# Gating and adding the last expert results: VectorE alone, or VectorE and ScalarE

## The chip, the cores and the metric

The kernel runs on one core of a Trainium2 chip. The metric is the device time of one execution in microseconds (us). Six runs of the kernel before gave a median of 709.76 us (706.66 to 710.63).

A core has five engines with instruction queues of their own: TensorE (PE in the profile, its weight loads PEld), VectorE (DVE), ScalarE (ACT), GpSimd (POOL) and SyncE (SP, which here only issues transfers). They wait for each other and for DMA transfers by semaphores.

## What is computed

A "macaron" block over x, 8 sequences of 512 tokens of width 128, in float32: half a mixture of experts, attention, and half a mixture of experts again. The last line below is the one that the change belongs to.

```
def ffn(x):                                   # 8 experts, each token goes to 2
    logits = einsum('bsd,de->bse', x, router_w) + router_b
    topk_scores, topk_idx = top_k(logits, 2)
    topk_gates = softmax(topk_scores, axis=-1)
    combine = einsum('bsk,bske->bse', topk_gates, one_hot(topk_idx, 8))
    ...                                       # over the experts:
        h = relu(einsum('bsd,df->bsf', x, w1) + b1)        # 128 -> 512
        y = einsum('bsf,fd->bsd', h, w2) + b2              # 512 -> 128
        acc = acc + y * combine_e[..., None]

x = x + 0.5 * ffn(layernorm(x))
x = x + attention(layernorm(x))               # 16 heads of 8, causal
x = x + 0.5 * ffn(layernorm(x))
```

Every token thus receives two results of the second mixture of experts, one from each of its two experts. Each is multiplied by the token's gate for that expert, and both are added to x. The gates already hold the factor 0.5.

## The kernel before

All of x stays on the chip: `x[b]` is a tile of 128 partitions x 4 x 128 for sequence b. Token t*128 + p of the sequence is in partition p, at index t. "A tile of tokens" below is one such t: 128 tokens, one in each partition, 128 values each.

**The groups.** The tokens go through the mixtures of experts in groups. The first mixture has the groups f0, f1 and f2, the second g0, g1 and g2. A group's tokens are routed, normalised and scattered to a buffer in HBM by expert; the experts then fetch their rows, and the results go back to HBM. For g1 and g2 they go there by the token's own place (`send`, L981, by indirect transfers of GpSimd): the buffer `ys` holds for every token two neighbouring rows, the results r = 0 and r = 1.

**The shares of g2.** g2 is the last group. Its tokens lie in four shares: tile 3 of sequence 4, and all four tiles of the sequences 5, 6 and 7. That makes 13 tiles of tokens.

**The order.** The kernel is written as generators, which a plan calls in turn. Attention of all 8 sequences, the experts of the groups and the routing are woven together. The order of the instructions on TensorE, ScalarE, VectorE and SyncE is the order in which they are called. When the last experts of g2 are through, only `collect` is left to do, for the four shares of g2:

```
last = [m.collect(g2, i, out, parts=min(2, g2.shares[i][2] - g2.shares[i][1])) for i in range(4)]
step(*last)
run(*last)
```

`step` takes each of the four generators up to its first `yield`: SyncE issues all loads. `run` then runs the generators one after the other to their end: the arithmetic, and the stores.

**`collect`.** It reads the two rows of every token of a share from `ys` to a tile `yr` (128 partitions x tiles x 2 x 128), in `parts` pieces. For the one-tile share parts is 1, and there is one load; for the others parts is 2, so n is 2, and there are two loads of two tiles of tokens each. All in all seven loads (L1140). Then, for each tile of tokens and for r = 0 and r = 1, VectorE does one fused operation (L1144, `scalar_tensor_tensor`): yr times the gate, a column of one value for each partition, plus x, into x. After the last tile of a part, SyncE stores that part of x to the output (L1150): seven stores. Two shares each use one buffer, `pair`, which stands under the tag "ee" in a pool of two.

The groups before g2 use `collect` as well (g1, with parts = 1), or `combine` (L1098), and have the rest of the kernel to run beside.

After the last store each engine reads a flag, `bad` (L1577), and jumps over a general path (L1581), which runs only for inputs that the fast path can't hold.

Of the kernel before, what the change touches and what calls it, by code (L numbers as in the profile page):

```python
# [14 lines left out]
AF = mybir.ActivationFunctionType  # L15
ALU = mybir.AluOpType
# [471 lines left out]
class Main:  # L488
# [638 lines left out]
    def collect(self, g, i, dst, parts=1):  # L1127

        nc = self.nc
        b, first, end = g.shares[i]  # L1130
        x = self.x[b]
        gates = self.ways[g.key[0], b][2]
        if i % 2 == 0:
            self.pair = self.p2.tile([P, 2, T, 2, D], FP, tag="ee", name=f"yr_{b}")
        yr = self.pair[:, i % 2]
        src = g.ys[: 2 * P * g.tiles, :].rearrange("(t p r) d -> p t r d", p=P, r=2)
        n = -(-(end - first) // parts)
        for t in range(first, end, n):
            rows = slice(t - first + g.base[i], t - first + g.base[i] + n)
            nc.sync.dma_start(yr[:, t : t + n], src[:, rows])  # L1140
        yield
        for t in range(first, end):
            for r in range(2):
                nc.vector.scalar_tensor_tensor(  # L1144
                    x[:, t, :], yr[:, t, r], gates[:, t, r : r + 1], x[:, t, :],
                    ALU.mult, ALU.add,
                )
            if (t - first) % n == n - 1:
                part = slice(t + 1 - n, t + 1)
                nc.sync.dma_start(  # L1150
                    dst[b].rearrange("(t p) d -> p t d", p=P)[:, part], x[:, part]
                )
            if parts == 1:
                yield
# [474 lines left out]
```

## Time and profile before

| | us |
|---|---|
| median of six runs | 709.76 |
| lowest and highest run | 706.66, 710.63 |
| the profiled execution, its whole time | 708.01 |
| its span, from the first instruction to the last | 706.3 |
| TensorE busy | 623.1 (88% of the span) |
| VectorE busy | 406.2 (58%) |
| ScalarE busy | 341.7 (48%) |
| GpSimd busy | 295.0 (42%) |

The granted clock of TensorE was 0.975 of its full speed on average.

How such a profile is read: the profile page has the busy share of each engine in 40 equal slices of the span, one digit for each slice, in tenths. The groups put together the instructions of one line, engine and shape: output, inputs and sizes, how often they ran, then busy time and the mean ns of one, and how long the engine was idle just before them and for whom. The timeline lists instructions in the order of time: start, duration, engine, line, operation. Equal ones in a row are merged, with their number at the end. The chain that ended last goes back from the last instruction of the span to what released it, and so on; its pieces are shown with start and duration. "issue" in it is time in which the engine waited for nothing that the profile shows. The table by windows has for each stretch the busy time and number of instructions of the engines PE, PEld, DVE, ACT and POOL, then the clock of TensorE, the mean share of time in which the core's 16 DMA engines were busy, and the GB/s that they moved.

### The profile page before, as it was taken

What the parts mean: (1) busy time and instruction counts of PE and PEld (TensorE: products, weight loads), DVE (VectorE), ACT (ScalarE), POOL (GpSimd) and SP (SyncE); (2) the same over time, 40 slices, a digit from 0 to 9 for tenths busy, and PEclk for the clock granted to TensorE, in tenths of its full rate; (3) what the DMA queues carried; (4) which work ended last, traced back from release to release, by engine and by line L of the source; (5) the groups of instructions that cost most, each with busy time, mean ns of one, the idle gap of its engine ahead of it and who ended that gap; (6) DMA issues with size and microseconds to landing.
All of it is one profiled execution on the core that took longest, in us unless ns stands there. A gap on an engine that the chain in (4) does not pass through costs nothing.

```text
span 706.3 us, 12906 instructions
## 1 busy us (share of the span) xinstructions
PE 623.1 (88%) x4797; PEld 403.2 (57%) x4797; DVE 406.2 (58%) x1432; ACT 341.7 (48%) x552; POOL 295.0 (42%) x318
## 2 busy tenths in 40 slices
PE   3269979989999999999999999989999988779970
PEld 2148856755656656555656556455465556647760
DVE  6636437644466575675676677767665644233424
ACT  4024443355565656466566565666646532234420
POOL 3744627643132214315054324332244455645550
PEclk9999999999999999999999999999999998979995
DMA  8746843221518961011211101012112121244224
GB/s 263 190 134 200 214 109 93 67 62 53 121 27 128 179 218 37 23 26 46 65 32 50 46 25 38 27 35 80 46 32 62 31 58 38 71 118 131 78 67 150
DMA packets 80229, 61.32 MB, mean 87 GB/s; under 512 B 7400, under 2 KB 73888, under 8 KB 80160
## 3 DMA queue, kind: packets, MB, share of 16 engines
q1 hardware_dynamic: 71296, 42.79, 24.2%
q0 software_dynamic: 8576, 17.63, 8.4%
q8 instruction: 40, 0.66, 0.4%
q14 instruction: 29, 0.24, 0.1%
q10 hardware_dynamic: 288, 0.01, 0.0%
HBM read 26.21 MB, written 34.19 MB: 86 GB/s over the span
## 4 chain that ended last, share of the span: by engine, by line
PE 81%; DVE 5%; ACT 3%; DMA 2%; another core or an unknown queue 2%; issue 2%; POOL 0%; POOLq 0%; SPq 0%; ACTq 0%
PE st L1231 13%; PE y_f L1037 11%; PE o L1257 11%; PE z_f L1013 11%; PE z_g L1013 10%; PE y_g L1037 9%; PE qkv_ps_a L1169 3%; PE qT_ps L1208 2%; PE otok_ps L1275 2%; PE kT_ps L1208 2%; PE xbT_ps_g L1000 2%; PE xbT_ps_f L1000 1%; ACT ee L1238 1%; DVE x L1144 1%
## 5 line engine op out<-in xcount | busy, mean ns | idle before, releaser
L1238 ACT ACTIVATE ee<-st 128x768 f32<-128x768 f32 (+1 forms) x192 | 159.0, 881 | 97.1 <-PE st L1231 84.3
L479 POOL DMA_INDIRECT yt_f<-ys,back_f x64 | 65.1, 1017 | 132.2 <-DVE ee L1245 56.7
L1245 DVE TENSOR_TENSOR ee<-ee,keep 128x256 f32<-128x256 f32 (+1 forms) x192 | 93.4, 507 | 22.7 <-ACT ee L1238 21.6
L1037 PEld LDWEIGHTS y_f<-w_sb,h_f 128*120 128x120 f32 (+1 forms) x704 | 86.0, 182 | 30.0 <-issue 17.1
L1231 PE MATMUL st<-qT,kT 32*128 32x512 f32 (+3 forms) x1024 | 96.1, 467 | 6.7 <-ACT kT L1214 4.3
L895 POOL DMA_INDIRECT xs<-xn_g,to_g x64 | 63.7, 995 | 87.5 <-DVE ee L1245 33.6
L1037 PEld LDWEIGHTS y_g<-w_sb,h_g 128*128 128x128 f32 x640 | 81.6, 193 | 32.5 <-issue 25.9
L1037 PE MATMUL y_f<-w_sb,h_f 128*120 128x128 f32 (+1 forms) x704 | 94.4, 277 | 1.4 <-ACT h_f L1020 1.1
L1013 PE MATMUL z_g<-xT_g,w_sb 128*128 128x512 f32 (+1 forms) x192 | 89.5, 552 | 6.4 <-ACT xT_g L1004 6.4
L1013 PE MATMUL z_f<-xT_f,w_sb 128*128 128x480 f32 (+1 forms) x192 | 89.3, 553 | 1.0 <-ACT xT_f L1004 1.0
L1257 PE MATMUL o<-ee,vpad 128*32 128x512 f32 (+3 forms) x1024 | 89.4, 442 | 0.8 <-DVE ee L1245 0.8
L1020 ACT ACTIVATE h_f<-z_f,b1T 128x480 f32<-128x480 f32 (+1 forms) x86 | 53.5, 625 | 71.6 <-PE z_f L1013 52.4
L1037 PE MATMUL y_g<-w_sb,h_g 128*128 128x128 f32 x640 | 86.1, 280 | 0.6 <-DVE o_tok L1280 0.3
L981 POOL DMA_INDIRECT ys<-ysb_g,home_g x64 | 62.7, 980 | 55.2 <-ACT h_g L1020 16.8
L1020 ACT ACTIVATE h_g<-z_g,b1T 128x512 f32<-128x512 f32 (+1 forms) x77 | 49.3, 642 | 53.4 <-PE z_g L1013 45.6
L1041 DVE TENSOR_TENSOR ysb_g<-y_g,b_sb 128x128 f32<-128x128 f32 x80 | 23.0, 290 | 85.3 <-PE y_g L1037 62.2
L1041 DVE TENSOR_TENSOR ysb_f<-y_f,b_sb 120x128 f32<-120x128 f32 (+1 forms) x88 | 25.0, 288 | 75.5 <-PE y_f L1037 62.5
L1231 PEld LDWEIGHTS st<-qT,kT 32*128 32x128 f32 x1024 | 43.1, 183 | 40.2 <-ACT kT L1214 12.8
L895 POOL DMA_INDIRECT xs<-xn_n,to_f x40 | 38.8, 971 | 36.8 <-issue 9.9
L1257 PEld LDWEIGHTS o<-ee,vpad 128*32 128x32 f32 x1024 | 23.5, 108 | 52.4 <-issue 6.6
L1013 PEld LDWEIGHTS z_g<-xT_g,w_sb 128*128 128x128 f32 x192 | 29.9, 194 | 26.2 <-issue 13.1
L1013 PEld LDWEIGHTS z_f<-xT_f,w_sb 128*128 128x128 f32 x192 | 30.5, 195 | 14.0 <-issue 8.5
(185 smaller groups left out, 770.7 us busy)
## 6 DMA issues: line engine op xcount, KB each, us to landing
xs<-zeros SPq DMA_DIRECT2D x8, 520.0 KB
xb_g<-xs SPq DMA_DIRECT2D x16, 260.0 KB
w_sb<-in_L_ffn_W_dram SPq DMA_DIRECT2D x16, 256.0 KB
xb_f<-xs SPq DMA_DIRECT2D x16, 240.0 KB
ys<-ysb_f SPq DMA_DIRECT2D x16, 240.0 KB
ys<-zeros SPq DMA_DIRECT2D x2, 1664.0 KB
x<-in_L_attn_x_dram SPq DMA_DIRECT2D x8, 256.0 KB
xs<-zeros SPq DMA_DIRECT2D x1, 1920.0 KB
```

The source lines that it names most:

```text
L479: ins = op(*args, **kw)
L895: ins = nc.gpsimd.indirect_dma_start(out=g.xs[:, :], out_offset=bass.IndirectOffsetOnAxis(ap=to[:, t, r : r + 1], axis=0), in_=xn[:, t, : ...
L981: ins = nc.gpsimd.indirect_dma_start(out=g.ys[:, :], out_offset=bass.IndirectOffsetOnAxis(ap=home[e][:rows, t : t + 1], axis=0), in_=ys[:r ...
L1013: nc.tensor.matmul(z[:, :n], self.w1_sb[:, e, ts(c, P)], xT[:, n0 : n0 + n], start=True, stop=True,)
L1020: ins = nc.scalar.activation(dst, z[:, :n], AF.Relu, bias=bias)
L1037: nc.tensor.matmul(y[:rows], h[:, c, ts(t, rows)], self.w2_sb[:, e, c, :], start=(c == 0), stop=(c == C - 1),)
L1041: ins = nc.vector.tensor_tensor(ys[:rows, t, :], y[:rows], self.b2_sb[:rows, e], ALU.add)
L1208: self.nc.tensor.transpose(tp[:, ts(t, P)], pad[:, t, 4 * g : 4 * g + 4, :].rearrange("p h s -> p (h s)"), self.ident,)
L1231: nc.tensor.matmul(st[:, h, c0 : c0 + N - kt * P], kT[r0 : r0 + SLOT, ts(kt, P)], qT[r0 : r0 + SLOT, kt * P :], start=True, stop=True,)
L1238: nc.scalar.activation(ee[:, two, :width], st[:, two, :width], AF.Exp)
L1245: ins = self.nc.vector.tensor_tensor(d, d, self.keep.unsqueeze(1).unsqueeze(1).to_broadcast([P, 2, len(parts), P]), ALU.min,)
L1257: self.nc.tensor.matmul(self.o[h * SLOT : (h + 1) * SLOT, kt * P :], self.vpads[b % 2][:, kt, 4 * g + h, :], ee[:, h, c0 : c0 + n], start= ...
```

## The change

For shares that come in two parts (three of g2's four, 12 of its 13 tiles), the result r = 0 is no longer gated and added by VectorE. ScalarE multiplies it by its gate, in place in `yr`. VectorE still gates and adds the result r = 1 of every tile with its fused operation. After the last tile of a part, one addition of VectorE brings both tiles' gated r = 0 results into x at once, and then the part is stored as before. The lone tile of sequence 4, and all that is collected earlier, have one part and stay as they were.

```
         for t in range(first, end):
-            for r in range(2):
+            if parts > 1:
+                nc.scalar.activation(
+                    yr[:, t, 0], yr[:, t, 0], AF.Identity, scale=gates[:, t, 0:1]
+                )
+            for r in range(parts > 1, 2):
                 nc.vector.scalar_tensor_tensor(
                     x[:, t, :], yr[:, t, r], gates[:, t, r : r + 1], x[:, t, :],
                     ALU.mult, ALU.add,
                 )
+            if parts > 1 and (t - first) % n == n - 1:
+                part = slice(t + 1 - n, t + 1)
+                nc.vector.tensor_tensor(x[:, part], x[:, part], yr[:, part, 0], ALU.add)
             if (t - first) % n == n - 1:
                 part = slice(t + 1 - n, t + 1)
                 nc.sync.dma_start(
```

## The prediction

> **What bounds the kernel now.** I read the page first: its slices say where the engines are busy, and with that whether the changed lines share their time with anything.
>
> ```profile
> span 706.3 us, 12906 instructions
> ...
> PE   3269979989999999999999999989999988779970
> ...
> DVE  6636437644466575675676677767665644233424
> ACT  4024443355565656466566565666646532234420
> ```
>
> Over most of the span TensorE is at 9 tenths. The last slice (688.6 to 706.3 us) is another stage: TensorE 0, ScalarE 0, VectorE 4 tenths. What is shortened there, and lies on the path that ends last, comes off the span whole. The timeline of the end shows the stage:
>
> ```profile
> 690.28 3.38 SPq L1140 DMA_DIRECT2D yr<-ys  x7
> 692.26 0.74 DVE L1144 SCALAR_TENSOR_TENSOR x<-yr,gates_g,x 128x128 f32<-128x128 f32 x2 [5.99 <-DMA yr<-ys]
> 693.76 8.53 SPq L1150 DMA_DIRECT2D out_dram<-x  x7
> 694.01 7.89 DVE L1144 SCALAR_TENSOR_TENSOR x<-yr,gates_g,x 128x128 f32<-128x128 f32 x24 [1.01 <-DMA yr<-ys]
> ```
>
> Seven loads, one lone tile (2 operations), then 24 operations without a wait for a transfer. These 24 are the 12 tiles of the three shares that have two parts, and the only instructions the change touches. The chain that ended last says whether they set the end, and at what pace:
>
> ```profile
> 690.68 3.30 DMA yr<-ys
> 693.98 0.03 issue
> 694.01 0.36 DVE x L1144
> 694.37 0.03 issue
> 694.39 0.62 DVE x L1144 x2
> 695.02 0.02 issue
> 695.04 0.62 DVE x L1144 x2
> ```
>
> They do. The second operation of a tile starts 0.38 us after the first (694.01, 694.39): it reads the x that the first wrote, and waits for it. The next tile's first operation needs nothing of that, and the tile after starts 0.65 us after this one (694.39, 695.04), so the step without a wait is 0.65 - 0.38 = 0.27. A part of two tiles is 1.30, six parts are 7.8, and the last ends at 701.89. What follows hangs on it: in the trace the last store issues at 701.92 and lands at 704.01, VectorE tests the flag `bad` at 702.17, and has its next instruction at 705.22, 1.1 us before the end.
>
> **The change, part by part.** Prices come from the groups with shapes kept apart:
>
> ```profile
> L844 DVE TENSOR_TENSOR gt_f<-gt_f,eq_f 128x256 f32<-128x256 f32 x8 | 3.4, 426 | 0.3
> L1144 DVE SCALAR_TENSOR_TENSOR x<-yr,gates_g,x 128x128 f32<-128x128 f32 x52 | 17.2, 348 | 7.9 <-DMA yr<-ys 7.0
> L1020 ACT ACTIVATE h_g<-z_g,b1T 128x256 f32<-128x256 f32 x17 | 8.1, 482 | 4.5 <-PE z_g L1013 4.4
> L929 ACT ACTIVATE ex_g<-ex_g 128x32 f32<-128x32 f32 x8 | 1.8, 230 | 2.8 <-DVE more_g L918 2.8
> L723 ACT ACT_TABLE_LOAD x1 | 1.3, 1283 | 1.7 <-PEq L1612 1.7
> ```
>
> *VectorE.* Twelve fused multiply-adds (r = 0) go; twelve stay, and now the two of a part are on different tiles, so the second doesn't wait: 0.27. Six additions of 128x256 come. Each waits for the second product: 0.38, as in the chain. The same form exists, in place and from two SBUF operands: 0.426. Successors that don't wait start some 0.08 before the end of the one before (0.348 against 0.27), so the next part starts 0.426 - 0.08 = 0.34 after the addition. A part costs 0.27 + 0.38 + 0.34 = 0.99 instead of 1.30. First start 694.01; the last addition starts at 694.01 + 5 x 0.99 + 0.65 = 699.61 and ends at 700.04. Against 701.89 that is 1.85 us less.
>
> *ScalarE.* Twelve activations of 128x128, scaled by a column, in place. ScalarE is idle from 681.4 on, so the cover is whole. No row has the form. Below: 0.230 (128x32). Above: 0.482 (128x256, with a bias column). I take the straight line between them at 128 columns, 0.34, as the form lies between in size and has one column operand. Two per part, overlapped by 0.1 us as the copies of L1172 and L1173 are in the trace (386 ns, next start after 268): done 0.24 + 0.34 = 0.58 after the load lands, and some 0.03 to pass on, so 694.62. VectorE's addition is ready at 694.01 + 0.65 = 694.66: no stall. At 0.482 it is 694.90, a stall of 0.24 in the first part alone, since ScalarE then takes 0.48 to 0.86 per part against VectorE's 0.99: gain 1.6. At 0.230 nothing changes. If ScalarE needed more than 0.55 per activation it would set the pace.
>
> The Trainium skill, "ScalarE: Activation LUTs", section "What ACT_TABLE_LOAD costs", gives an activation 186 ns, 93 for each column operand and 0.833 per element; by it this one is an estimated 0.386 us, and the first part would stall by 0.05. The same page, "Rules for kernel authors", wants multiplications on VectorE and not on ScalarE; by the per-element price that is right here too, but it speaks of one operation alone, and here ScalarE has nothing else to do.
>
> *Queues.* On ScalarE nothing stands behind the twelve but its test of `bad` and its way out, which it passed at 681.2 us and now reaches at about 699; VectorE's comes a microsecond later, so it isn't the last. Its first activation also waits for the lone tile's load, an old load and VectorE's earlier work, all past by 693.0. SP's order is unchanged: seven loads, then seven stores, each behind its part's last VectorE operation; they move up by 0.27 (first part) to 1.85 (last).
>
> *Transfers.* With VectorE faster, the loads are next in line:
>
> ```profile
> 693.00:693.50 0.50, 0.00 (x0) 0.00 (x0) 0.00 (x0) 0.00 (x0) 0.00 (x0) 0.50 1.06 373
> ...
> 697.50:698.00 0.50, 0.00 (x0) 0.00 (x0) 0.47 (x3) 0.00 (x0) 0.00 (x0) 0.50 0.99 295
> 698.00:698.50 0.50, 0.00 (x0) 0.00 (x0) 0.47 (x2) 0.00 (x0) 0.00 (x0) 0.50 0.31 89
> ```
>
> The second to last column is the share of the DMA engines: they are full from 692.5 to 698.0. By the trace's landings the six loads arrive at 693.98, 694.64, 695.32, 696.63, 697.32 and 697.99. The new starts of the parts are 694.01, 695.00, 695.99, 696.98, 697.97 and 698.96: margins of 0.35 us at the tightest (fourth), 0.97 at the last. One store more (128 KB, 0.45 us at 290 GB/s) gets in among the loads; it falls to the last ones, where the margin holds it. ScalarE needs 0.58 after each landing and VectorE reaches the addition 0.65 after its start, so it holds there too. Cover gone, a load late by 0.5 beyond its margin costs that 0.5.
>
> **Sum.** The profiled execution took 708.01 us, 706.3 of them its span: 706.3 - 1.85 = 704.4, so 706.2. It lies 1.75 below the median of the six runs, 709.76; the stage is the same work in each, so I carry the difference over: 707.9. Bounds of the unknown price: 1.6 to 1.85 us.
>
> **Rivals.**
>
> *Late data.* ScalarE or the loads set the pace. For it: the saturated DMA engines and margins of 0.35 us; a table load for the new function of 1.28 (the row above), if it had to come behind the landed load, would delay every addition by about that. Against: the landings are 0.80 apart on average, less than 0.99, and Relu, copy and Exp share one table load in this trace. It leaves a gain of 0.5 to 1: 709.0. The skill, same page, section "Table sets: the hidden batching unit", has identity in every set, and so no load at all; a switch would be 2.66 us by it.
>
> *Slower: two ways out collide.* ScalarE now leaves about 1.4 us before VectorE instead of 20. VectorE's jump over the unused general path takes 3.05 us in the trace (702.17 to 705.22), TensorE's 3.4. If ScalarE's takes as long and VectorE's has to wait behind it, up to 3.4 come on top: 709.76 - 1.85 + 3.4 = 711.3; it decides from 1.85 us of delay. Against: ScalarE's own jump took 0.45 (681.22 to 681.67).
>
> *No effect.* The end hangs on something else, such as the stores' landing. Then 709.8. Against: store and VectorE's jump both start within 0.3 us of the last addition. That the change reaches other tiles than these twelve is excluded: a share of one tile, and all collected earlier, keep one part.
>
> *More.* VectorE's jump, whose target moves with its stream, takes part of its 3.05 no longer: 1.5 more, 706.4.
>
> **How the numbers follow.** Forecast 0.68, late data 0.10, collision 0.11, no effect 0.05, more 0.06. A measurement can tell about 0.3% from no change, 2.1 us. The forecast, 0.26%, lies just inside, and medians of runs that scatter over 4 us fall on either side of the bound. Five of the six runs are longer than the profiled one; what of that is VectorE's waiting in this stage shrinks as well, so I lean a little outward: 0.38 faster, 0.30 same. With "more" (0.06) and 0.02 of late data, faster is 0.46; same is 0.30 + 0.08 + 0.05 = 0.43; slower 0.11. The forecast's own range is 706.9 to 709.0 (gain 1.6 to 1.85, and about 1 us for two medians); to hold 8 in 10 it reaches down to "more" and up past no effect: 705.9 to 710.5.
>
> **What would show it.** In the last stage: 14 fused operations, six additions of 128x256 at about 0.43, a part every 0.99 us, and twelve activations at about 0.34. VectorE idle before the first addition: under 0.1 beyond its step (0.24 at most). Last VectorE work ends near 700.04, the seven stores' issues span 6.7 us instead of 8.53, span 704.4. Wrong, if additions wait for ScalarE or a first product for its load in later parts, if a table load stands before the first activation, or if VectorE's way out takes more than 3.1 us.

## The result and the profile after

The changed kernel's median is 706.98 us (36 runs, 702.61 to 711.88), beside 708.52 us before (78 runs, 704.54 to 714.85). The ratio is 0.9987, with a 95% interval of 0.9975 to 0.9999: 0.9 us less, between 0.1 and 1.8. The two medians themselves are 1.54 apart. The prediction had 1.85 us less. The time lies in its range and the direction is right, but by the ratio the gain is about half of what was forecast; how much of the 1.85 is missing the times alone can't say. The forecast time, 707.9, started from the median of six runs, 709.76, which 78 runs put at 708.52.

The profiled execution of the changed kernel took 706.54 us. Its page, the span and the slices:

```profile
span 704.8 us, 12921 instructions
...
PE   3269989989999999999999999989999988779980
...
DVE  6636437645456675675687677767665645133423
ACT  4034343355665665566475565656646532234422
```

ScalarE's last slice has 2 tenths where it had 0, and VectorE's 3 where it had 4. The stage is the same one, and the timeline shows what became of it (start, duration, engine, line, operation; in brackets the idle time before, and what ended it):

```profile
689.57 3.38 SPq L1140 DMA_DIRECT2D yr<-ys  x7
691.68 0.74 DVE L1148 SCALAR_TENSOR_TENSOR x<-yr,gates_g,x 128x128 f32<-128x128 f32 x2 [6.67 <-DMA yr<-ys]
692.79 0.61 DVE L1148 SCALAR_TENSOR_TENSOR x<-yr,gates_g,x 128x128 f32<-128x128 f32 x2 [0.37 <-DMA yr<-ys]
692.93 1.29 ACT L1144 ACTIVATE yr<-yr,gates_g 128x128 f32<-128x128 f32 x4 [12.80 <-DMA yr<-ys]
693.05 7.52 SPq L1157 DMA_DIRECT2D out_dram<-x  x7
693.65 0.42 DVE L1154 TENSOR_TENSOR x<-x,yr 128x256 f32<-128x256 f32 x1 [0.25 <-ACT yr L1144]
693.99 0.61 DVE L1148 SCALAR_TENSOR_TENSOR x<-yr,gates_g,x 128x128 f32<-128x128 f32 x2
694.70 0.42 DVE L1154 TENSOR_TENSOR x<-x,yr 128x256 f32<-128x256 f32 x1
695.81 0.61 DVE L1148 SCALAR_TENSOR_TENSOR x<-yr,gates_g,x 128x128 f32<-128x128 f32 x2 [0.68 <-DMA yr<-ys]
...
696.58 0.42 DVE L1154 TENSOR_TENSOR x<-x,yr 128x256 f32<-128x256 f32 x1 [0.16 <-ACT yr L1144]
696.92 0.61 DVE L1148 SCALAR_TENSOR_TENSOR x<-yr,gates_g,x 128x128 f32<-128x128 f32 x2
697.63 0.43 DVE L1154 TENSOR_TENSOR x<-x,yr 128x256 f32<-128x256 f32 x1
697.98 0.61 DVE L1148 SCALAR_TENSOR_TENSOR x<-yr,gates_g,x 128x128 f32<-128x128 f32 x2
698.69 0.42 DVE L1154 TENSOR_TENSOR x<-x,yr 128x256 f32<-128x256 f32 x1
699.03 0.61 DVE L1148 SCALAR_TENSOR_TENSOR x<-yr,gates_g,x 128x128 f32<-128x128 f32 x2
699.74 0.42 DVE L1154 TENSOR_TENSOR x<-x,yr 128x256 f32<-128x256 f32 x1
```

From the first part's start (692.79) to the end of the last addition (699.74 + 0.425, 700.17) are 7.38 us. Before it was 694.01 to 701.89, 7.89. This stretch is called the stage below. So 0.51 us come from the stage in this pair of executions, not 1.85. The rest of the 1.5 us between the two spans comes ahead of the changed instructions, and is taken as chance here: the first load is issued 0.7 us earlier (689.57 against 690.28), behind instructions that are the same in both kernels, and the first part's load lands 3.2 us after that issue instead of 3.7. What follows the last addition took 0.26 us longer (4.68 against 4.42).

The starts of the parts show where the missing time lies. The six starts are 692.79, 693.99, 695.81, 696.92, 697.98 and 699.03. A part that waits for nothing takes 1.05 (697.98 to 699.03). The first takes 1.20, and its addition was kept waiting by ScalarE for 0.25 (in the brackets). The second takes 1.82, because the third part's first product waits 0.68 for its load. Five parts at 1.05 and a last one of 1.14 to its end are 6.40; 0.15, 0.76 and 0.07 on top, for parts one to three, make the 7.38.

The groups of the stage, with shapes kept apart (count, then busy time and mean ns of one, then idle time before):

```profile
L1148 DVE SCALAR_TENSOR_TENSOR x<-yr,gates_g,x 128x128 f32<-128x128 f32 x14 | 4.4, 347 | 7.8 <-DMA yr<-ys 7.7
L1144 ACT ACTIVATE yr<-yr,gates_g 128x128 f32<-128x128 f32 x12 | 4.0, 393 | 14.5 <-DMA yr<-ys 12.8 <-DVE x L1154 1.6
L1154 DVE TENSOR_TENSOR x<-x,yr 128x256 f32<-128x256 f32 x6 | 2.5, 425 | 0.8 <-ACT yr L1144 0.4
```

Counts and durations are as predicted for VectorE (14 and 6, 0.35 and 0.43). An activation is 0.39 us and not 0.34. The time is not in the operations but between them, and the chain of waits of the changed kernel shows one such place (DVEq is VectorE's sequencer):

```profile
697.63 0.43 DVE x L1154
698.06 0.53 DVE x L1148 x2
698.59 0.03 issue
698.62 0.02 DVEq L1154
698.64 0.04 issue
698.69 0.42 DVE x L1154
```

The addition waits for two things, the product before it and ScalarE. One of the two waits stands as a step of its own in VectorE's queue, and costs some 0.06 us even where ScalarE was done long before: the addition starts 0.71 us after the part's first product (697.98 to 698.69) and not 0.65.

The load that came late is seen in the windows too. First the changed kernel, then the kernel before, each about 4 to 5 us after its first load's issue; the last two columns are the share of the DMA engines and the GB/s:

```profile
693.50:694.00 0.50, 0.00 (x0) 0.00 (x0) 0.35 (x2) 0.50 (x3) 0.00 (x0) 0.50 1.27 229
694.00:694.50 0.50, 0.00 (x0) 0.00 (x0) 0.50 (x3) 0.22 (x1) 0.00 (x0) 0.50 0.75 166
694.50:695.00 0.50, 0.00 (x0) 0.00 (x0) 0.40 (x2) 0.00 (x0) 0.00 (x0) 0.50 0.93 303
```

```profile
694.00:694.50 0.50, 0.00 (x0) 0.00 (x0) 0.46 (x2) 0.00 (x0) 0.00 (x0) 0.50 0.82 272
694.50:695.00 0.50, 0.00 (x0) 0.00 (x0) 0.50 (x2) 0.00 (x0) 0.00 (x0) 0.50 0.80 268
```

The engines are as busy, but move 166 to 229 GB/s in that microsecond instead of 270. The third part's load landed 6.21 us after the first issue, against 5.03 in the first profile of before.

### The profile page after: what moved, and what is told of

The parts are those of the page before. It is cut to its first block, busy times and chain, and to the rows that moved or that the text cites. A ratio compares the mean times of both kernels' runs of the same rounds, so it can differ in the third digit from the quotient of the medians.

```text
span 704.8 us, 12921 instructions
## 1 busy us (share of the span) xinstructions
PE 624.0 (89%) x4797; PEld 402.7 (57%) x4797; DVE 404.5 (57%) x1426; ACT 345.3 (49%) x564; POOL 295.6 (42%) x318
## 5 line engine op out<-in xcount | busy, mean ns | idle before, releaser
L1013 PE MATMUL z_g<-xT_g,w_sb 128*128 128x512 f32 (+1 forms) x192 | 91.0, 561 | 6.4 <-ACT xT_g L1004 6.4
```

The costliest lines, as they stand in the source:

```text
L1013: nc.tensor.matmul(z[:, :n], self.w1_sb[:, e, ts(c, P)], xT[:, n0 : n0 + n], start=True, stop=True,)
```

## The experiments

Two theories were put to the test. W: once VectorE is faster, the loads of `yr` set the pace. S: the late load was chance, and what the prediction missed are longer steps. The first four kernels ran on one chip, the others on two more.

**The changed kernel once more** (no edit).

> The changed kernel unaltered, for a second profile of its last stage. Theory W (the loads of yr set the pace once VectorE is faster): again at least one first product of a part waits more than 0.3 us for its load, and the stage from the first part's start to the end of the last addition is 7.0 us or more (7.38 in the first profile, 7.89 before the change); ratio to before about 0.9985. Theory S (the late load was chance; what was missed are longer steps: 1.05 us a part instead of 0.99, and 0.2 us for ScalarE in the first part): no first product waits over 0.1 us from the second part on, the stage is about 6.6 us, ratio 0.998 to 0.999.

The median was 706.86 us in 12 runs, the ratio 0.9973 (0.9947 to 1.0). The stage was 7.05 us. From the timeline of this execution:

```profile
694.62 0.42 DVE L1154 TENSOR_TENSOR x<-x,yr 128x256 f32<-128x256 f32 x1
695.39 0.61 DVE L1148 SCALAR_TENSOR_TENSOR x<-yr,gates_g,x 128x128 f32<-128x128 f32 x2 [0.34 <-DMA yr<-ys]
```

Again it is the third part that waits for its load, for 0.34 us instead of 0.68. That fits W, with little room: expected were over 0.3 us of wait and 7.0 or more.

**Operations in turns, without ScalarE** (the edit in outline).

```
-    for r in range(2):              # for each tile t
-        x[t] += yr[t, r] * gate[t, r]
+    for r in range(2):              # for each part of two tiles
+        for t in part:
+            x[t] += yr[t, r] * gate[t, r]
```

> The kernel before the change, with one thing altered: in the parts of two tiles VectorE does both r = 0 operations, then both r = 1, so that none waits for the one before it. ScalarE takes no part. By the steps of the profile (0.27 without a wait) a part costs 4 x 0.27 = 1.08 us instead of 1.30, the stage 6.6 us instead of 7.89: 1.3 us less if the loads allow it, ratio 0.998. Theory W: the loads don't allow it, some first product waits over 0.3 us for its load, the gain is 0.5 to 1.0, about that of the changed kernel. Theory S: the gain is 1.3 or more than the changed kernel's, as there is no ScalarE to wait for.

The timeline:

```profile
695.66 2.19 DVE L1150 SCALAR_TENSOR_TENSOR x<-yr,gates_g,x 128x128 f32<-128x128 f32 x8 [0.32 <-DMA yr<-ys]
...
698.02 4.29 DVE L1150 SCALAR_TENSOR_TENSOR x<-yr,gates_g,x 128x128 f32<-128x128 f32 x16 [0.17 <-DMA yr<-ys]
```

Eight operations in 2.19 us, sixteen in 4.29: 0.27 each, no wait among them. The stage is 6.65 us, with 0.17 of idle time before the third part's load, which makes 0.25 lost, as an operation that doesn't wait starts 0.08 before the end of the one before. This is 1.24 less than before, more than the changed kernel gained in either profile so far, without any help from another engine. The times can't confirm it: 708.41 us in 12 runs, ratio 1.0001 (0.9973 to 1.0029), an interval of 4 us. In VectorE's steps, taking away the wait between r = 0 and r = 1 is thus worth about as much as the whole change (1.24 + 0.25, beside the 1.48 of the next two runs), without moving any work.

**The arithmetic with the loads out of the way**, in both forms. The loads read the buffer of group g1, which is ready long before, so they are issued early (the first at 676.81 and not at 690.28 in the form before); the output is not the block's. The cut line goes on as before (`...`).

```
-        src = g.ys[: 2 * P * g.tiles, :].rearrange(...)
+        src = (self.ys[3] if g.key == "g2" else g.ys)[: 2 * P * g.tiles, :].rearrange(...)
```

> The kernel before the change, with the last seven loads reading the same rows of the buffer of group g1 instead of g2's own, which hold the results of other tokens: the last additions don't have the right data, but all work is there. These loads can then be issued long before the last experts end, and VectorE's last 26 operations wait for no transfer. Both theories: one run of 26 operations behind the last ysb, 8.5 us (0.74 + 7.8), no idle time for a DMA. It is the base for the next run.

> The changed kernel with the same early loads of g1's rows. No load and no ScalarE to wait for: 2 operations, then six parts of 1.05 us, 0.74 + 6.4 = 7.1 us. Theory W: the difference to the run before (early_before) is 1.4 us in VectorE's last stage and about as much in the time, more than the 0.9 of the real pair, because what took the rest of the gain, the loads, is gone. Theory S: 1.4 us as well in VectorE's stage, but the real pair differs by as much too (a gain of 0.9 would then be a matter of the measurement, and after_again shows a stage of 6.6).

The timelines, first of the form before the change, then the end of the changed one, whose run began at 684.22:

```profile
688.47 8.53 DVE L1144 SCALAR_TENSOR_TENSOR x<-yr,gates_g,x 128x128 f32<-128x128 f32 x26
```

```profile
684.22 1.26 DVE L1148 SCALAR_TENSOR_TENSOR x<-yr,gates_g,x 128x128 f32<-128x128 f32 x4
...
690.85 0.42 DVE L1154 TENSOR_TENSOR x<-x,yr 128x256 f32<-128x256 f32 x1
```

8.53 us against 7.05 (684.22 to 691.27), lone tile included: 1.48 us less, as both theories had it. ScalarE's twelve activations had ended by 682.7 here, so neither a load nor ScalarE is waited for, and an addition still starts 0.71 us after its part's first product. So 1.4 to 1.5 is what the change is worth in VectorE's queue, not 1.85. The times, 703.76 and 700.27 us with ratios of 0.9932 (0.9903 to 0.9961) and 0.9897 (0.9861 to 0.9933) to the kernel before, differ by 3.5 us. That is more than the stage explains; ten and four runs are few, and the stage also started at other points in the two profiles (688.47 and 684.22).

**The kernel before once more** (no edit).

> The kernel before, unaltered, for a second profile of its last stage. Theory W (loads set the pace only for a faster VectorE): with 1.30 us a part VectorE falls behind the loads, so no first product but the first waits for a load, and the stage from the first part's start to the end of the last addition is again 7.8 to 7.9 us, whatever the loads do. From the issue of the first load to the first part's landing 3.1 us, as in the three other profiles (the first profile of before had 3.7); to the end of the last addition then 11.0 us, against 10.6 and 10.2 in the changed kernel's two profiles. If it is 11.6 again, the gain inside the stage is larger than the 0.5 to 0.9 read so far.

```profile
697.01 7.89 DVE L1144 SCALAR_TENSOR_TENSOR x<-yr,gates_g,x 128x128 f32<-128x128 f32 x24 [0.69 <-DMA yr<-ys]
```

7.89 us again, to the hundredth. In this execution the third part's load landed 5.93 us after the first issue, nearly as late as in the changed kernel's first profile (6.21), and cost nothing: at 1.30 us a part VectorE reached it only at about 3.5 + 2 x 1.30 = 6.1. So the late load isn't something that the change brings about. The old pace hid it. The first part's landing was 3.4 us after the first issue, the end 11.35 after it, between the 11.0 that was expected and the 11.6 of the first profile.

**Loads from two queues.**

```
-            nc.sync.dma_start(yr[:, t : t + n], src[:, rows])
+            queue = nc.scalar if parts > 1 and t == first else nc.sync
+            queue.dma_start(yr[:, t : t + n], src[:, rows])
```

> The changed kernel, with the first load of each two-part share issued by ScalarE's queue, the others by SyncE's. The seven issues then take about 1.9 us instead of 3.4. Theory W: the third part's load, issued a microsecond earlier, lands earlier than 5.5 us after the first issue, its first product waits less than 0.3 us, the stage is 6.6 to 6.9 us. Rival (the DMA engines are full, and the issues are ahead of them anyway): the last load lands at 7.7 to 8.3 us after the first issue as before, and some part waits over 0.3 us again; the stage is 7.0 or more.

The third part landed 5.20 us after the first issue, the last at 7.04, no product waited, and the stage was 6.48 us (6.6 to 6.9 were expected).

> The kernel turns (VectorE alone, r = 0 of both tiles, then r = 1) with the loads issued from two queues as in after_two_queues. A part needs 1.08 us. Theory W: what turns lost to loads (0.32 us in the first part, 0.17 in the third) shrinks, the end of the last operation comes 9.4 us or less after the first load's issue, against 9.8 in turns. Rival: full DMA engines, 9.8 again.

Here the third part landed at 4.57. The stage was 6.39 us and the end 9.50 us after the first issue. The same kernel, run again with timing:

> turns_two_queues again, now timed: VectorE alone, without ScalarE, loads from two queues. Its profile ended 9.5 us after the first issue, against 11.4 to 11.6 before and 10.2 to 10.6 in the changed kernel. Both theories: 1.9 us less than before, ratio 0.997 to 0.998, better than the changed kernel by about 0.9 us; the runs scatter by 4 us, so this may stay unclear.

In this execution the third part landed at 5.92, the stage was 7.26, the end 10.24 us after the first issue; 708.07 us in 12 runs, ratio 0.9995 (0.9969 to 1.002). So the expectation of 9.5 did not hold: earlier issues don't keep a load from being late, and the first two profiles with two queues showed more favourable landings than this one.

**Additions one part later.** Each addition, with its store, is emitted behind the next part's two products (in outline).

```
+    def finish():
+        x[part] += yr[part, 0]; store x[part]
+    if self.later_add is not None:
+        self.later_add()
+    self.later_add = finish
```

> The changed kernel, with each addition of 128x256 put behind the next part's two products, so that it waits neither for ScalarE nor for the product before it. VectorE's own work for a part falls to 0.27 + 0.27 + 0.34 = 0.88 us. Theory S (VectorE's steps are what counts): no wait for loads from the second part on, stage 5.6 to 5.8 us. Theory W: VectorE waits for loads in two or more parts, and the end comes 1.1 to 1.4 us after the last landing: about 9.0 to 9.6 us after the first load's issue, stage 6.0 to 6.4.

```profile
697.81 0.61 DVE L1149 SCALAR_TENSOR_TENSOR x<-yr,gates_g,x 128x128 f32<-128x128 f32 x2 [1.26 <-DMA yr<-ys]
...
698.68 0.61 DVE L1149 SCALAR_TENSOR_TENSOR x<-yr,gates_g,x 128x128 f32<-128x128 f32 x2
...
699.54 0.61 DVE L1149 SCALAR_TENSOR_TENSOR x<-yr,gates_g,x 128x128 f32<-128x128 f32 x2
```

VectorE's own pace is 0.86 us a part (698.68 to 699.54). The third part landed at 6.03 and its product waited 1.26 us; the stage was 6.76, the end 9.93 us after the first issue. A VectorE that comes there sooner waits longer for the same load. The form of it that W expected, two or more parts waiting and the end 1.1 to 1.4 behind the last landing, did not come: behind the first part only the third waited, and the end is 1.8 behind the last landing (8.09). The stage is longer than either theory had it (5.6 to 5.8, and 6.0 to 6.4).

**Stores held back.** The aim was to see whether the stores slow the loads. In outline:

```
+    self.held_stores.append(store)      # for g2, instead of the store itself
     ...
     run(*last)
+    for store in m.held_stores:
+        store()
```

> The changed kernel, with the seven stores of the last stage issued after the last addition instead of one by one. It is to tell why the third part's load lands late (5.8 to 6.2 us after the first issue, with its neighbours at 7.2 to 8.3 for the last). Theory C (stores among the loads slow them): without stores the third part lands by 5.1, its first product waits less than 0.1 us, the last load lands by 7.4. Rival H (the loads alone do it; the trace has stores moving data only after 6 us): the third part lands at 5.4 or later and its product waits 0.3 us or more. Either way the end comes late, as the stores' issues, 7 x 0.4 = 2.6 us, now stand behind the arithmetic.

The edit does not do this. SyncE has nothing but these stores behind the loads, each store waits for its own addition, and so the order on every engine is that of the changed kernel: this is a third execution of it. So whether stores slow the loads wasn't tried. The data of the stores is excluded in another way: in the trace of the changed kernel its packets (512 B each) begin 6 us after the first load's issue, behind the slow stretch at 4 to 5. The issue of the first store is not: it stands at 3.5 us in every execution with one queue, whether the third load then lands at 4.7 or at 6.2. As a third execution it is the most telling one:

```profile
693.54 0.61 DVE L1149 SCALAR_TENSOR_TENSOR x<-yr,gates_g,x 128x128 f32<-128x128 f32 x2 [0.43 <-DMA yr<-ys]
...
695.80 0.61 DVE L1149 SCALAR_TENSOR_TENSOR x<-yr,gates_g,x 128x128 f32<-128x128 f32 x2
...
699.68 0.43 DVE L1155 TENSOR_TENSOR x<-x,yr 128x256 f32<-128x256 f32 x1
```

The third part (695.80) waits for nothing: its load landed at 4.72. The stage is 6.56 us, which is theory S's number.

**Both alterations together**, twice.

> Both alterations of the changed kernel together: additions one part later, and loads from two queues. VectorE needs 0.88 us a part. In after_two_queues the third part landed at 5.2 and the last at 7.0 us after the first issue; so theory W puts the end of the last addition at 5.2 + 3.9 = 9.1 us after the first issue (9.5 in after_two_queues, 10.2 to 10.6 in the changed kernel, 11.4 to 11.6 before), which is 2.3 us less than before: ratio 0.9965 to 0.997, if the runs can tell. If the end is at 9.5 again, VectorE's steps were not what was left.

> later_two_queues unaltered, for twelve more timed runs and a second profile. Its first profile ended 8.9 us after the first load's issue, 2.6 less than before, which would be a ratio of 0.9963; its twelve runs gave 0.9985 (0.9965 to 1.0006). If the 2.6 is what the version is worth, these runs fall below 0.998; if 0.9985 or more comes again, the load's landings take part of it back in most executions, and the profile's end is at 9.2 to 9.9.

In the first profile the third part landed at 4.61, the stage was 5.74 and the end 8.87 us after the first issue. In the second these were 4.55, 6.53 and 9.60; the second part's load came late (0.68 us of wait) and so did the fourth's (0.42). In both, what follows the last addition took 5.0 us, where it was 4.4 to 4.5 before. The times: 707.28 us, ratio 0.9985 (0.9965 to 1.0006), and 707.56 us, ratio 0.9982 (0.9955 to 1.0009). Each interval holds 1, and both hold the changed kernel's 0.9987; 0.9982 lies between the two outcomes that the second expectation told apart. On time, no version was shown to beat it.

The stages side by side. "Third load" is its landing after the first load's issue:

| kernel | third load, us | stage, us |
|---|---|---|
| before | 5.03 | 7.89 |
| before, again | 5.93 | 7.89 |
| changed | 6.21 | 7.38 |
| changed, again | 5.81 | 7.05 |
| changed, third execution (stores_last) | 4.72 | 6.56 |
| changed, two queues | 5.20 | 6.48 |
| changed, additions later | 6.03 | 6.76 |
| changed, both alterations | 4.61 | 5.74 |
| changed, both alterations, again | 4.55 | 6.53 |
| turns | 5.47 | 6.65 |
| turns, two queues | 4.57 | 6.39 |
| turns, two queues, again | 5.92 | 7.26 |

## Why the prediction was right, and where it was off

*That the last stage is bare, and all of it on the path:* right. VectorE's additions set the end before and after, and the way out behind the last addition stayed about as long (4.4 and 4.5 us before, 4.5 to 4.7 after).

*VectorE's own part, 0.99 us, gain 1.85:* the kind of gain is right, the size wrong. Measured is 1.05 us a part. The step that failed is "Each waits for the second product: 0.38, as in the chain". The chain before had operations that wait for one thing. The addition waits for two, and the second wait costs 0.06 us each time, in six parts 0.37 us. With the loads and ScalarE out of the way the two forms differ by 1.48, which is 1.85 less 0.37.

*ScalarE:* the activation was put at 0.34 us and is 0.39. The Trainium skill's figure ("ScalarE: Activation LUTs", "What ACT_TABLE_LOAD costs"), an estimated 0.386, was nearer than my line between two rows. ScalarE's first activation also starts 0.14 us after VectorE's first product, though both wait for the same load (692.93 and 692.79): three more waits, for things long past, stand before it in its queue. The prediction named them and gave them no price. The addition of the first part came 0.15 us later for it than a part's step would put it, inside the bound of 0.24.

*Transfers:* this is the step whose result was wrong. "Margins of 0.35 us at the tightest (fourth)" was read from the landings of one execution. The engines were not quite full there either: from 694 to 695 their share is 0.82 and 0.80, at 270 GB/s, in the stretch where the third part's load is late elsewhere. For the third part the margin was 0.67; the load came late by 0.68 in the first profile of the changed kernel, 0.34 in the second, and not at all in the third. The landing of that load varies from 4.72 to 6.21 us over the executions with one queue, and from 4.55 to 5.92 with two. An operation that starts when the new VectorE wants it (about 3.2 + 0.15 + 2 x 1.05 = 5.5) meets that spread in the middle; the old one, which wanted it at 6.1 and 6.3, came behind it in both profiles. Two of the prediction's own signs of being wrong came with it: a first product that waits for its load in a later part, and there an addition that waits for ScalarE (0.16, third part).

*The sum:* the three executions of the changed kernel have stages of 7.38, 7.05 and 6.56, on average 7.00, which is 0.9 less than 7.89. The ratio of the timed runs says 0.9 (0.1 to 1.8) as well, but three stages that differ by 0.8 make so close an agreement partly luck. From the first issue to the end of the last addition it is 11.61 and 11.35 before, and 10.60, 10.20 and 9.85 after: 1.3 less on average, of which 0.4 is the first part's load landing sooner, ahead of the change. Of the 1.85 forecast for the stage, some 0.5 went to steps that were priced too short (0.37 for the second wait, 0.15 for ScalarE) and 0.4 on average to late loads (0.76, 0.42 and 0). The forecast's mechanism held, but the size in the stage is that of the rival "late data" (a gain of 0.5 to 1), which had 0.10; less than half of what makes it so is the loads, and no table load stood before the activations.

*The other rivals:* "collision" did not happen. ScalarE's jump over the general path took 2.5 us in the trace of the changed kernel (698.43 to 700.97) instead of 0.45, but VectorE's still ended last: it took 3.18 there (700.56 to 703.74), and 3.00 and 3.02 in the other two executions, against 3.04 and 3.07 before. That excludes "more" as well, as the jump didn't lose 1.5 us. "No effect" is excluded by the stages.

*Faster or the same:* the gain of 0.13% is below the 0.3% that was called measurable. That lies in the case "same", which had 0.43, and "faster" had 0.46; the lean towards faster, from the longer runs among the six, was not borne out. In the two profiles of the kernel before it is the time ahead of the stage that differs, not the stage: TensorE's last matmul ends at 685.1 and 687.4 us, and the stage is 7.89 in both.

What stays open is why single loads come late. In the slow stretch some 1 KB packets of these loads take 0.3 to 0.9 us in the changed kernel's trace, where most take 0.05. Kernels without ScalarE's work show it too (turns with two queues, again: 5.92), so that isn't its cause, and the stores' data isn't, as its packets come later. It isn't one chip either: a third load at 5.8 or later was seen on each of the three. Memory that is read just after it was written isn't needed for slow packets: in the trace of the form before with early loads, whose rows were written over 16 us earlier, eight 1 KB packets of the seven loads took 0.3 to 0.88 us, though other transfers ran beside them there. Whether it adds to the delay in the last stage isn't shown.

## What to carry to other kernels

Price a wait by how many things the instruction waits for: here a second semaphore was a step of its own in the queue, 0.06 us each time, and an activation on an idle engine paid 0.14 us for three old waits that it had collected. Before moving work to another engine, see whether the operations merely wait for each other; writing the same operations in another order gave as much in this stage as the second engine, though its timed runs (ratios 1.0001, and 0.9995 with two queues) neither show such a gain nor rule it out. And a margin against transfers must be read from several executions: a load's landing that varied by 1.5 us cost nothing as long as the consumer was slow, and up to 0.76 us of the gain when it was not.

## What was not expected of the hardware

- Seven loads of 128 and 256 KB, issued in the same order at the same intervals, land differently each time: the third 256 KB load at 4.7 to 6.2 us after the first issue in three executions of the same instructions. Each load reports its landing in sixteen pieces, and the last one can be far behind: in "changed, again" fifteen had landed by 4.75 us and the sixteenth at 5.81.
- The same jump over the unused code took ScalarE 0.45 us when it came there 20 us early, 2.5 to 2.9 us right after the activations, and 5.2 and 4.8 us in the two executions of turns with two queues, where it came right after issuing loads.
- Execution times scatter by some 10 us (704.54 to 714.85 in 78 runs of the kernel before), yet the stage of that kernel, which waits for no load once it has begun, repeats to 0.01 us in two profiles. A microsecond in one stage is read from a few profiles better than from twelve timed runs, whose interval is 3 to 4 us.
